# A recommender kernel on one core: masking gathered rows, sharing the last pooling product, two store queues, and another place for eight key transposes

## The chip, the core and the metric

The kernel runs on one core of a Trainium2 chip. A core has five instruction queues that run side by side[...]: TensorE (PE in the profile, with its weight loads shown as PEld), VectorE (DVE), ScalarE (ACT), GpSimd (POOL) and SyncE (SP), which here only issues DMA transfers. ACT and POOL can issue transfers as well. The metric is the device time of one execution in microseconds (us); lower is better.

## What is computed

A batch of 1024 users, each with a history of up to 100 items of 128 numbers, is scored in four parts. Cut to what matters here:

```python
keys = scan(gru_step, h0, history)              # 100 steps, one state of 128 per user and step
score = mlp(concat(keys, q, keys - q, q * keys))  # q: the item; layers of 80, 40, 1, relu
attn = softmax(where(mask == 1, score, -inf), axis=1)
pooled = einsum('bt,btd->bd', attn, keys)       # (users, 128)
att_seq = pooled.T[:100]                        # feature t of pooled weights step t below

def augru_step(h, (x_t, a_t)):                  # x_t: keys of step t, a_t: att_seq[t]
    r = sigmoid([h, x_t] @ Wr)
    u = sigmoid([h, x_t] @ Wu)
    h_hat = tanh([h * r, x_t] @ Wh)
    u = a_t * u
    return (1 - u) * h + u * h_hat

state = aug_seq[length - 1]                     # the state at each user's last step
out = mlp(concat(user, item, hist, item * hist, state))   # 200, 80, 1, sigmoid
```

The second recurrence needs `pooled`, which needs the softmax over all 100 steps, so it can't begin before the first recurrence has ended. A weight `a_t` of zero leaves a state as it is: the kernel therefore sets the weights at and after a user's length to zero, and the last state is then the one that is asked for.

## The kernel before

The batch lies in two halves of 512 users (`HB`), features on the 128 partitions. The work has two phases, and in each of them the order of instructions on every engine is the order in which the code emits them.

The first phase (`gru_phase`) loops over the 100 steps. In each step it runs the GRU of both halves, the attention network of an earlier step (`attend`, matrix products on PE into PSUM, and `take`, which adds the item's part `q0` on DVE and applies relu on ACT), a piece of an online softmax and a piece of the pooling (`pool`). Both networks' products are cut into 32-column pieces, so that four run side by side in the array. Scores go by a small DMA from a row of `mv` to a tile `s_b`, where DVE transposes them. The softmax works in blocks of steps, whose ends are `ENDS` (the last are 93, 96, 98, 100); each block has three stages, `scores(0)`, `tops` and `sums`, which the function `stage` takes from a list. Pooling multiplies the keys of a step by their weights and adds the product to `pooled`; within the loop GpSimd does this. Other instructions of the loop that take no part of the recurrence are handed out one piece for each step by the generator `load_later` (among them a sort of the users by length, whose result is the index tile `idx`).

After the loop comes a tail that is written out by hand (L915 to L987). It finishes the attention of steps 98 and 99 (`take(T - 2)` to `take(T + 1)`), the last three softmax blocks, the pooling (half 0 on GpSimd, half 1 on DVE) and eight pieces of the final network's first layer (`some`, L922). At its end (L976) DVE multiplies each half of `pooled` by the mask of lengths, `used`, into a tile `t`; SP stores the first 32 features to `pooled_d[0]` and the other 96 to `pooled_d[1]` (those of half 1 here, those of half 0 on ACT's queue at L1402).

The second phase (`augru_phase`) is built in three versions for different distributions of lengths. A value in memory, `over_d`, is read by each engine, and a branch (L1475, L1476) selects one. It sorts the users: the stored keys, and the weights in `pooled_d`, are read back with gathers on GpSimd (`load_row` for keys, `gather_weights` for the first 32 weights), indexed by `idx`. Its steps alternate between the halves (`half_step(t, i)`): PE closes the gates r and u with the state, ACT applies sigmoid, DVE multiplies, PE closes the gate h, ACT applies tanh, and PE opens the three gates of the next step with the next key. Some of the things that precede the steady alternation:

- keys of steps 0 to 3 are gathered early as rows (`rows[0, i]`) and transposed on PE by `load_key`, each followed by a copy on ACT;
- `first_step` computes step 0's gates u and h, which depend on the key alone;
- `open_gates(1, 1)` and `open_gates(1, 0)` open six gates;
- `first_state(i, p)` spreads the weights of step 0 over all partitions by a product with the identity (`weight_row`) and sets the state to weight times u times h; `first_weights` spreads those of step 1; `store_weights` transposes all 32 and stores them to `att_d`, from where each later step reads its own by `load_att`.

```python
def first_state(i, p):
    weight_row(0, i, p)
    u, h = gates[i]
    nc.vector.tensor_mul(p, p, u)
    nc.vector.tensor_mul(h3[i], p, h)
```

## Time and profile before

| what | value |
|---|---|
| median of 3 runs | 2014.82 us (2014.07 to 2015.9) |
| the profiled execution's own time | 2014.8 us |
| its span in the profile | 2013.0 us |
| PE busy | 1986.5 us, 99% of the span |
| DVE, ACT, POOL busy | 83%, 46%, 63% |
| mean TensorE clock granted | 0.993 |

The span runs from the first to the last instruction of the program; the execution's own time has 1.8 us around it. The page gives PE as busy nearly throughout, and within the loop of the first phase, and within the steps of the second, its instructions follow each other without a gap. The 40 slices of the page are 50 us each, too wide for the passage from one phase to the other, which lies near 1380 to 1440 us; tables of shorter stretches and instructions in order of time show it. In those, an instruction's line is start, duration, engine, line of the code, operation, output and inputs; square brackets give the idle time before it and what ended it. Matrix products of this kernel in fp32 appear as two records for each instruction.

### The profile page before, as it was taken

Reading aid. Unit: us, or ns where it says so; the run is one execution under the profiler, and the core shown is the slowest. Engines: PE = TensorE matmul, PEld = TensorE weight load, DVE = VectorE, ACT = ScalarE, POOL = GpSimd, SP = SyncE. Lnnn points to the kernel's source line nnn. Section 1 sums busy time; section 2 is a strip of 40 time slices with the busy share of each in tenths; the row PEclk is TensorE's granted clock in tenths of the full one; section 3 lists DMA queues with packets and bytes.
Section 4 is the critical chain, followed back from the end, with each engine's and each line's share of the span. In section 5 each row is a group of like instructions: output and inputs, shape, how many; then the busy total and the mean of one; then the engine's idle time right before and its main releaser. Section 6 shows DMA issues by size and latency. Waiting matters only on the chain.

```text
span 2013.0 us, 40935 instructions
## 1 busy us (share of the span) xinstructions
PE 1986.5 (99%) x15324; PEld 992.8 (49%) x15324; DVE 1672.2 (83%) x3017; ACT 935.5 (46%) x1679; POOL 1277.1 (63%) x1325
## 2 busy tenths in 40 slices
PE   9999999999999999999999999998899999999998
PEld 2345555555433333333333333334444556678997
DVE  7878999887978887888878898998487777888985
ACT  4444454454444454444444454453334444445553
POOL 0233939669796959595887868898674354445331
PEclk9999999999999999999999999999899999999998
DMA  4442333323334334333333333333343343333331
GB/s 124 98 117 91 107 103 103 92 83 104 115 112 102 120 107 121 115 112 102 111 98 96 107 104 94 107 96 106 102 127 101 97 110 98 93 105 95 85 78 30
DMA packets 242075, 204.84 MB, mean 102 GB/s; under 512 B 59506, under 2 KB 204890, under 8 KB 241866
## 3 DMA queue, kind: packets, MB, share of 16 engines
q1 hardware_dynamic: 227514, 169.37, 30.1%
q0 software_dynamic: 12480, 32.04, 5.7%
q8 instruction: 122, 2.00, 0.4%
q14 instruction: 87, 0.71, 0.1%
q10 hardware_dynamic: 1872, 0.72, 0.1%
HBM read 146.01 MB, written 54.41 MB: 100 GB/s over the span
## 4 chain that ended last, share of the span: by engine, by line
PE 95%; DVE 3%; issue 1%; ACT 1%; ACTq 0%; DVEq 0%
PE ps L534 49%; PE pm L700 17%; PE pr L1131 4%; PE ph L1131 4%; PE pu L1131 4%; PE pr L1127 4%; PE ph L1127 4%; PE pu L1127 4%; PE pr L1204 0%; PE ph L1204 0%; PE p L1324 0%; DVE pu L1155 0%; PE pu L1030 0%; PE pd L243 0%; DVE ps L564 0%
## 5 line engine op out<-in xcount | busy, mean ns | idle before, releaser
L534 PE MATMUL ps<-x,wih 128*32 128x512 f32 x4800 | 775.9, 593 | 0.0
L534 PE MATMUL ps<-hn,whh 128*32 128x512 f32 x4752 | 769.6, 592 | 1.4 <-ACT hn L582 1.4
L534 PEld LDWEIGHTS ps<-x,wih 128*32 128x32 f32 x4800 | 259.0, 110 | 302.0 <-issue 299.1
L534 PEld LDWEIGHTS ps<-hn,whh 128*32 128x32 f32 x4752 | 257.0, 110 | 298.7 <-issue 294.6
L519 POOL TENSOR_TENSOR xm<-x,m 128x512 f32<-128x512 f32 x200 | 236.7, 1183 | 142.2 <-DMA m<-mask_d 82.5
L546 ACT ACTIVATE r<-ps,brz 128x512 f32<-128x512 f32 x200 | 137.5, 688 | 388.4 <-PE ps L534 388.2
L520 POOL TENSOR_TENSOR hist<-hist,xm 128x512 f32<-128x512 f32 x200 | 257.9, 1289 | 15.7
L700 PE MATMUL pm<-hn,wk 128*32 128x512 f32 x1200 | 266.4, 592 | 0.1
L700 PE MATMUL pm<-kq,wkq 128*32 128x512 f32 x1200 | 265.8, 592 | 0.0
L188 POOL DMA_INDIRECT rows<-keys_d,idx_k x218 | 211.4, 970 | 81.4 <-POOL rows L187 46.7
L637 POOL TENSOR_TENSOR pooled<-pooled,kw 128x512 f32<-128x512 f32 x191 | 246.0, 1288 | 15.0
L636 POOL TENSOR_TENSOR kw<-kt,e 128x512 f32<-128x512 f32 x191 | 206.3, 1080 | 70.7 <-DVE e L809 70.6
L565 ACT ACTIVATE ps<-ps,bih 128x512 f32<-128x512 f32 x200 | 132.4, 662 | 225.9 <-DVE ps L564 225.9
L554 DVE SCALAR_TENSOR_TENSOR u<-ps,bhh,r 128x512 f32<-128x512 f32 x198 | 147.6, 746 | 73.2 <-PE ps L534 70.5
L1139 ACT ACTIVATE c<-ph,bh 128x510 f32<-128x510 f32 (+57 forms) x174 | 88.1, 507 | 258.8 <-PE ph L1131 221.3
L700 PE MATMUL pm<-mv,w 128*32 128x512 f32 (+1 forms) x808 | 196.3, 592 | 0.8 <-DVE e L790 0.8
L569 DVE TENSOR_TENSOR d<-hn,ps 128x512 f32<-128x512 f32 x198 | 136.1, 687 | 35.9 <-ACT ps L565 35.5
L570 DVE TENSOR_TENSOR d<-ps,d 128x512 f32<-128x512 f32 x200 | 138.3, 692 | 28.4 <-ACT ps L566 14.0
L187 POOL COPY rows<-rest 128x1 f32<-128x1 f32 x202 | 38.3, 190 | 193.0 <-DVE rest L1168 182.9
L582 ACT COPY hn<-ps 128x512 f32<-128x512 f32 x200 | 116.4, 582 | 92.8 <-DVE kq L576 91.0
L564 DVE TENSOR_TENSOR ps<-ps,u 128x512 f32<-128x512 f32 x200 | 140.0, 700 | 22.4 <-PE ps L534 1.5
L571 DVE TENSOR_TENSOR ps<-ps,d 128x512 f32<-128x512 f32 x200 | 139.9, 699 | 6.8
(228 smaller groups left out, 3120.4 us busy)
## 6 DMA issues: line engine op xcount, KB each, us to landing
x<-in_hist_x SPq DMA_DIRECT2D x210, 256.0 KB
keys_d<-kt SPq DMA_DIRECT2D x48, 1024.0 KB
m<-mask_d SPq DMA_DIRECT2D x200, 128.0 KB
rows<-keys_d,idx_k POOLq DMA_INDIRECT x218
s_b<-mv SPq DMA_DIRECT2D x200, 8.0 KB
keys_d<-kt SPq DMA_DIRECT2D x32, 64.0 KB
mask_i<-in_mask SPq DMA_DIRECT2D x8, 200.0 KB
part_d<-part SPq DMA_DIRECT2D x2, 400.0 KB
```

The source lines that it names most:

```text
L188: nc.gpsimd.indirect_dma_start(out=r[:, at, :], out_offset=None, in_=keys_d[q], in_offset=bass.IndirectOffsetOnAxis(ap=idx_k[:, k, i : i + ...
L519: nc.gpsimd.tensor_mul(d, x, m)
L520: nc.gpsimd.tensor_add(acc, acc, d)
L534: nc.tensor.matmul(p[ts(q, R), :], lhsT=w[:, g, ts(q, R)], rhs=v, start=(j == 0), stop=(j == len(parts) - 1),)
L554: nc.vector.scalar_tensor_tensor(out=u, in0=ph, scalar=bhh[:, 2:3], in1=r, op0=ALU.add, op1=ALU.mult,)
L564: nc.vector.tensor_add(pi, pi, u)
L571: nc.vector.tensor_add(pi, pi, d)
L636: eng.tensor_mul(d, k, w)
L637: eng.tensor_add(acc, acc, d)
L700: nc.tensor.matmul(p[i][s, :], lhsT=w[:, s], rhs=v, start=start, stop=stop)
L1127: nc.tensor.matmul(p, lhsT=m[:, 1, :], rhs=k, start=True, stop=False)
L1131: nc.tensor.matmul(p, lhsT=m[:, 0, :], rhs=v, start=False, stop=True)
```

## The change

It is a bundle of seven edits, all of them around the passage from the first phase to the second.

1. The item's part of the attention network at steps 98 and 99 is added by PE (six more instructions in `attend`), and `take` no longer adds it on DVE; ACT reads PSUM itself.
2. In `sums` of the block that ends at 96, the weights are copied to PSUM first, and the sum of the block and the old sum are made from the copy. The copy that the tail made for DVE's pooling goes.
3. The tail's order: feature pieces are issued later, pooling of half 1 is done in smaller portions between the softmax stages, two early key gathers instead of three come before the last block.
4. DVE takes the last multiplication of half 0's pooling (`product`); GpSimd only adds it.
5. Keys 0 and 1 are transposed, and step 0's gates computed, in the tail and not behind the branch. Key 0 goes to `h3`, key 1 to `hist`, the gates to `item` and `s_bs`.
6. The first 32 features are stored unmasked, straight from `pooled`, by two queues (half 1 by SP, half 0 by ACT). Their mask is applied behind the gather, in `first_state`, from a mask `used_s` in sorted order that is made in the loop; for it a third number, the length, goes through the sort. The other 96 features are masked as before, but stored in step 2 of the second phase, by SP.
7. Keys 2 and 3 are transposed inside steps 1 and 2; `first_weights` of half 0 and the order in step 1 move with them.

```diff
-    idx = const.tile([P, GH, NH * 2], I32, name="idx")
+    idx = const.tile([P, GH, NH * 3], I32, name="idx")
+    used_s = const.tile([P, NH, GH, R], U8, name="used_s")
...
+            nc.gpsimd.tensor_copy(ids[:, :, 2], len_i)
...
+            for i in range(NH):
+                sorted_len = pre.tile([P, GH], F32, name="sorted_len")
+                nc.scalar.copy(sorted_len, idx[:, :, 3 * i + 2])
+                nc.vector.tensor_tensor(
+                    out=used_s[:, i],
+                    in0=sorted_len.unsqueeze(2).to_broadcast([P, GH, R]),
+                    in1=step[:, :R].unsqueeze(1).to_broadcast([P, GH, R]),
+                    op=ALU.is_gt,
+                )
+            yield
...
+            def product(self):
+                e, n, t = self.todo.pop()
+                d = wp.tile([P, KH, R], F32, tag="kw", name="kw")
+                w = e[1][:, self.ks, n].unsqueeze(2).to_broadcast(d.shape)
+                nc.vector.tensor_mul(d, self.kt[t // G][:, :, t % G, :], w)
+                self.todo.append((d, None, t))
...
+            def query(i, *groups):
+                for q in groups:
+                    pack(i, q, wq[i], item[:, halves[i].cols], False, False)
+
             for turn in range(2 * NH):
                 i, j = divmod(turn, 2)
+                if j and T - 2 <= t < T:
+                    query(i, 0, 1)
+                    if i:
+                        query(1, QB[1])
+                        query(0, QB[0])
...
-                if t < T:
+                if t < T - 2:
                     sums.append(wp.tile([P, HB], F32, name="f"))
                     nc.vector.tensor_add(sums[-1], p[half.i], q0[:, half.cols])
...
-                nc.vector.tensor_reduce(den_n, e[:, :, :n], AX.X, ALU.add)
+                f, old = e, None
+                if banks and both[1] is None:
+                    b = banks["e"][0]
+                    f = soft["copy"] = b[:, : NK * rows].rearrange("p (k n) -> p k n", n=rows)
+                    old = b[:, HB - NK :]
+                    nc.vector.tensor_copy(f, e[:, :, :rows])
+                nc.vector.tensor_reduce(den_n, f[:, :, :n], AX.X, ALU.add)
...
         exponents()
         some(0, 1)
-        some(2, 3)
+        some(2)
         take(T - 1)
-        some(2, 3)
+        some(2)
         attend(T)
-        some(4)
+        some(3)
...
         take(T)
-        some(4)
+        some(3)
         attend(T + 1)
-        some(5, 6)
+        some(4, 5)
         stage()
+        exponents()
         take(T + 1)
-        exponents()
-        some(5, 6)
-        some(7)
+        some(4, 5)
+        some(6, 7)
+        halves[1].pool(1, nc.vector)
+        stage()
+        halves[0].pool(T, nc.gpsimd)
+        gather_early(2)
+        halves[1].pool(2, nc.vector)
+        some(6, 7)
+        for n in range(2):
+            for half in halves:
+                k = (h3[half.i], hist[:, half.cols])[n]
+                p = pa.tile([P, HB], F32, tag="a", name="pk")
+                for g in range(GH):
+                    nc.tensor.transpose(
+                        p[:, ts(g, P)], rows[0, half.i][:, g, ts(n, P)], ident
+                    )
+                nc.scalar.copy(k, p)
+                later["key", n, half.i] = k
         for half in halves:
             half.store((T - 1) // G)
-        halves[1].pool(T, nc.vector)
-        stage()
-        gather_early(3)
-        halves[0].pool(T, nc.gpsimd)
-        some(7)
         stage(2)
         exponents()
+        for half in halves:
+            gates = (item[:, half.cols], s_bs[NH * ((soft["j"] - 1) % 2) + half.i])
+            later["gates", half.i] = gates
+            for to, (n, f) in zip(gates, (("u", AF.Sigmoid), ("h", AF.Tanh))):
+                if half.i:
+                    p = banks["f"].pop(0)
+                else:
+                    p = pa.tile([P, HB], F32, tag="a", name=f"p{n}")
+                nc.tensor.matmul(
+                    p,
+                    lhsT=later["w" + n][:, 1, :],
+                    rhs=later["key", 0, half.i],
+                    start=True,
+                    stop=True,
+                )
+                nc.scalar.activation(to, p, f, bias=later["b" + n])
         stage()
+        halves[0].product()
         halves[0].pool(T, nc.gpsimd)
         halves[1].pool(T, nc.vector)
         gather_early(3)
-        for half in reversed(halves):
-            t = blocked(s_bs[NH * (soft["j"] % 2) + half.i])
-            nc.vector.tensor_mul(t, later["used"][:, half.ks, :], pooled[:, half.ks, :])
+        for half, eng in zip(reversed(halves), (nc.sync, nc.scalar)):
...
-            nc.sync.dma_start(out=first[0], in_=t[:R])
+            eng.dma_start(out=first[0], in_=pooled[:R, half.ks, :])
+            t = blocked(s_bs[NH * (soft["j"] % 2) + half.i])
+            nc.vector.tensor_mul(t, later["used"][:, half.ks, :], pooled[:, half.ks, :])
...
-        for to, t in later["att", 1]:
-            nc.sync.dma_start(out=to, in_=t)
...
             nc.vector.tensor_mul(p, p, u)
             nc.vector.tensor_mul(h3[i], p, h)
+            r = sorted_rows[i][:, :, 1:R]
+            nc.vector.tensor_mul(r, r, used_s[:, i, :, 1:])
...
-            if t == 1 and i == 0:
-                store_weights(0, pa.tile([P, HB], F32, tag="a", name="pw"))
-                first_state(1, spare)
-            elif t == 1:
-                first_weights(1, spare)
+            if t == 1:
+                first_weights(i, spare)
+                load_key(2, i)
...
             if t == 1 and i:
                 store_weights(1, spare)
+                load_key(3, 0)
+            elif t == 1:
+                open_state(1, 0)
+                store_weights(0, pa.tile([P, HB], F32, tag="a", name="pw"))
+                first_state(1, spare)
+            elif t == 2 and i == 0:
+                load_key(3, 1)
...
-        for i in range(NH):
-            load_key(0, i, (None, FREE_BANK)[i])
-        gates = [first_step(i) for i in range(NH)]
-        for i in range(NH):
-            load_key(1, i, (FREE_BANK, None)[i])
-        for to, t in later["att", 0]:
-            nc.scalar.dma_start(out=to, in_=t)
+        gates = [later["gates", i] for i in range(NH)]
+        keys.update({(1, i): later["key", 1, i] for i in range(NH)})
         sorted_rows = [gather_weights(i) for i in range(NH)]
-        for k in range(14, KH):
+        for k in range(13, KH):
             load_row(1, 0, k)
-        for i in range(NH):
-            load_key(2, i, (FREE_BANK, None)[i])
         open_gates(1, 1, EARLY_BANKS)
         open_gates(1, 0, LATE_BANKS)
-        for i in range(NH):
-            load_key(3, i)
         spare = bank("spare", EARLY_BANKS[-1])
         first_state(0, pa.tile([P, HB], F32, tag="a", name="first"))
-        first_weights(0, spare)
...
+                if t == FIRST[1] - 2:
+                    for to, of in later["att", i]:
+                        nc.sync.dma_start(out=to, in_=of)
```

## The prediction

> **What bounds the kernel now.** I read the page first: its span and the engines' shares of the chain that ended last.

> ```profile
> span 2013.0 us, 40935 instructions
> ...
> PE 95%; DVE 3%; issue 1%; ACT 1%; ACTq 0%; DVEq 0%
> ```

> TensorE carries 95% of the chain, and the change leaves nearly all its work in place. What can move is the rest, about 100 us of chain, and a table of stretches says where. Columns: busy us of PE, PEld, DVE, ACT, POOL with their counts, granted TensorE clock, DMA share, GB/s.

> ```profile
> 1340.00:1380.00 40.00, 40.00 (x369) 14.86 (x362) 36.90 (x57) 21.08 (x33) 36.80 (x32) 1.00 0.24 71
> 1380.00:1405.00 25.00, 19.97 (x111) 12.61 (x109) 20.69 (x49) 9.58 (x20) 19.32 (x20) 1.00 0.38 112
> 1405.00:1410.00 5.00, 1.94 (x8) 1.57 (x8) 4.35 (x14) 0.23 (x1) 4.84 (x5) 0.61 0.74 238
> 1410.00:1415.00 5.00, 3.84 (x5) 1.73 (x6) 4.79 (x8) 3.07 (x5) 4.70 (x5) 0.50 0.01 3
> ...
> 1428.00:1440.00 12.00, 8.84 (x36) 4.86 (x37) 5.83 (x9) 2.51 (x4) 3.99 (x5) 0.87 0.15 41
> 1440.00:1480.00 40.00, 40.00 (x106) 18.80 (x105) 29.72 (x50) 15.78 (x24) 30.05 (x52) 1.00 0.56 161
> ```

> Before 1380 and after 1440 PE is full. Between them DVE and POOL are full up to 1415, and PE works at half clock for part of it. So the change is worth what it takes from these 60 us. The timeline, engine by engine, shows the steps of the passage:

> ```profile
> 1388.35 1.29 DVE L734 TENSOR_TENSOR f<-pm,q 128x512 f32<-128x512 f32 x2 [2.55 <-PE pm L700]
> ...
> 1402.54 0.72 DVE L786 STREAM_TRANSPOSE last<-s_b 128x512 f32<-128x512 f32 x1
> ...
> 1414.71 1.29 DVE L978 TENSOR_TENSOR s_b<-used,pooled 128x512 f32<-128x512 uint8 x2
> 1429.23 0.70 DVE L1064 TENSOR_TENSOR first<-first,first_u 128x512 f32<-128x512 f32 x1 [13.22 <-PE first L1053]
> ```
> ```profile
> 1413.23 1.27 POOL L637 TENSOR_TENSOR pooled<-pooled,kw 128x512 f32<-128x512 f32 x1
> 1414.65 0.98 POOL L188 DMA_INDIRECT rows<-keys_d,idx_k  x1
> ...
> 1420.67 0.95 POOL L153 DMA_INDIRECT att_r<-pooled_d,idx  x1 [2.51 <-DMA pooled_d<-s_b]
> ```
> ```profile
> 1415.43 0.93 SPq L982 DMA_DIRECT2D pooled_d<-s_b  x2
> ```

> DVE is without a break from 1388.35; both poolings end near 1414.6; the mask follows, the two stores start at 1415.43, and the first weight gather waits for the second store until 1420.67. PE's `first` comes at 1427.83, 7.16 us after that gather, and PE is full again some 12 us later. The printed chain runs through PE's key transposes at 1407 to 1427 instead. Both end together: `first` waits for the last row gather of half 0 as well, by its own semaphore, so both branches have to become shorter.

> [...]

> ```profile
> L813 DVE TENSOR_TENSOR old<-den,e x13: 860/866/1023, 301.9 to 1391.2; 128x32 f32<-128x32 f32 x13
> L813 DVE TENSOR_TENSOR old<-den,last x2: 186/187/188, 1402.0 to 1406.4; 128x32 f32<-128x32 f32 x2
> ```

> The same tiny product takes 866 ns from SBUF beside GpSimd and 187 ns from PSUM. [...]ACT's branch at 1406.43 is followed by 3.53 us in which it does nothing, and PE's takes 6.9 us (1400.35 to 1407.28). [...]the table shows 0.50 at 1410 to 1415. [...]

> **The change, part by part.** Times are of the profiled execution (2014.8, practically the median 2014.82); the sum is a shift of PE's full phase.

> *Item part on PE.* 16 instructions become 22. Before, one `attend` at full packing takes 3.43 us: eight records of 0.43 us in each of four column groups. Groups 0 and 1 now hold twelve, so 5.13 us: +1.7 us for step 98 and again for 99. The second ran 5.76 us before (1382.49 to 1388.26), because it began before `mv` was there; now `mv` comes early. So PE ends it at 1381.3 + 2.9 (features) + 5.13 = 1389.3 and ACT's relu at about 1390.6, against 1390.3: +0.3. In exchange DVE loses 4 x 0.65 us of sums, and no longer waits 2.55 us for PE: `scores(0)` starts at 1381.7, the sums at 1386.4 against 1390.8.

> *Copy in PSUM.* L813 and L814 were 1.02 and 1.29 us here and become 0.19 each: -1.9 us on DVE. The copy (0.28) was there already.

> *Pooling order.* The next block's scores need `s_b`, landed at 1392.1 before (DVE came at 1395.8); now 1392.5, and DVE is ready: start at 1391.9. From there: scores and maxima 3.0, one product and sum 1.4, sums 1.1, five pooling instructions 3.6, so the last block starts at 1401.1, against 1402.54. It needs 3.0 to the exponent. ACT now has four key copies of 0.58 before that exponent, PE's features ending at 1401.8: it comes at 1404.75, +0.5. Then 0.3 for the exponent and 1.84 for the sums: 1406.95. `product` 0.7; seven instead of ten instructions of 0.7 for half 1: DVE ends at 1412.7 (before 1414.7, masked half 1 at 1415.4). POOL: 1.07 + 2.36 + 1.28, from 1407 at once: 1411.7 (before 1414.5).

> *Stores.* Each waited for a DVE mask of 0.69 us and for the other one on SP. Now one on each queue at 1412.75 and 1411.8. The first landed 2.7 us after issue, the second 3.8 with three others behind it. I take 2.7: 1415.45. Behind ACT's store, which waits for POOL's last sum, stand its branch and nothing needed before `first`. The big key stores (two of 1 MB, from 1398 to 1409 at 294 GB/s) now follow features and key copies on SP: 1402.6 to about 1411.5, just clear. POOL has three key gathers of 1.26 us first: 1415.4. With 0.8 us from landing to gather as before (1419.86 to 1420.67), the weight gather starts at 1416.2: **-4.45 us**. `first` at 1423.3.

> *PE before `first`.* Four transposes, four gate products and their ACT work (a table load of 1.28, four activations of 0.69) move into the wait for the pooling, free. After the gates (1407.8) PE branches, 6 to 7 us by the row above: 1414. Six openings, four at half clock (1.7) and two at 0.86: 1422.5. Cover 0.8 us, small.

> *From `first` to full PE.* Before: 17.87 us to the product pr of step 2 at 1445.70, of which the waits at 1429.9 to 1434.8, where PE's completions came late by up to 2.9 us beside an instruction fetch at 1432.4, and half-clock products at 1438 to 1440. New, engine by engine: state at +2.85, mask 0.25 (124 elements; nearest row L813 to L790, 0.2 to 0.9), r at +4.65 to 5.35, weights and rest to +7.6, `att_t` +8.25, state of half 1 at +9.7; PE then needs two products 1.7, weights 0.86, two key transposes 0.9, openings 2.6, `store_weights` 0.45, ph 0.86: +17.1. Gain 0.7. Key 3 of half 1 adds 0.45 in the full phase. An instruction fetch that falls into it again costs up to 3 (taken: 0, both ends kept)[...].

> *The rest.* Six stores in step 2 on SP (0.5 to 1.3 us each) stand before loads needed a step later, 10 us: 0. The used_s work in the loop is 4 tiny instructions under full PE; ACT waits once for DVE ahead of the next r: 0 to 0.7, taken 0.2. Fewer early gathers: the third row comes later, needed at 1460: 0.

> Sum: -4.45 - 0.7 + 0.45 + 0.2 = -4.5: 2014.8 - 4.5 = **2010.3 us**.

> **Rivals.** *PE late behind its branch* (23%): [...]the openings all run cold; `first` at 1426.5 and 3 us of the gain is gone: 2013.3. For it: 0.8 us of cover[...]. *The late completions don't return anywhere* (14%), neither here nor at 1388 (where they came 1.0 late), and step 98's products pack better than counted: 2 to 3 us more, 2007.8. *Stores in the way* (8%): [...] If the 2.4 MB move at half of the 294 GB/s, they last 17 us, to 1420, the weights land at 1423, gathers begin at 1424 and `first` comes at 1431: +3.2; with three key transposes of steps 1 and 2 exposed at 1.2 us each (0.44 on PE, 0.58 on ACT, two hand-overs) and the small terms, about 2021. It decides from a landing after 1420. That an edit doesn't do what it says is possible for `product`: it moves 1.07 us from POOL to DVE, and by my sum DVE ends last; without it DVE would end at 1412.0 and POOL at 1412.8, so it is worth nothing either way.

> **How the numbers follow.** My own case has 55%, with a range of 2008.8 to 2012.3[...]. About 0.2% (4 us, below 2010.8) is what this measurement tells from no change; of the 55%, 44 lie below. Faster 44 + 14 = 58%, same 11 + 23 = 34%, slower 8%. The range that holds 8 in 10 leaves out most of the slow case and the best of the fast one: 2007.8 to 2013.6.

> **What would show it.** `scores(0)` of the last block near 1401, the two pooled stores at 1412 to 1413 on two queues, the first weight gather near 1416, `first` near 1423 and the first opening of step 2's products without a late completion. Wrong if `first` waits for PE's openings, if pooled ends after 1414, or if landing takes over 4 us.

## The result, and the profile after

| series | before, median | changed kernel, median | ratio, 95% interval |
|---|---|---|---|
| first (14 and 14 runs) | 2014.85 us | 2012.76 us (2010.76 to 2014.21) | .9990 (.9983 to .9998) |
| second (39 and 19 runs) | 2013.12 us | 2011.24 us (2009.1 to 2014.74) | .9988 (.9981 to .9995) |
| third (47 and 13 runs) | 2005.38 us | 2005.52 us (2000.87 to 2007.02) | .9998 (.9990 to 1.0006) |

The forecast was 2010.3 us, 4.5 us below before. The first two series give 2 us, and the third, on another chip, nothing. The second and third series ran on chips that I call A and C; the first has the level of chip A and profiles like it. Four experiments ran on a chip B, where before takes 2004.94 us; the changed kernel itself did not run there. Of its 13 runs on chip C two took 2000.9 and 2001.3 us and the others 2004.4 to 2007.0, so a profile shows one outcome of several.

The first profile of the changed kernel is that of its fastest run of the first series (2010.76 us). Its page, span and chain by engine:

```profile
span 2009.0 us, 40971 instructions
...
PE 97%; issue 1%; DVE 1%; DMA 0%; ACT 0%; POOL 0%; another core or an unknown queue 0%; SPq 0%; ACTq 0%; DVEq 0%; POOLq 0%
```

The chain names PE with a larger share than before (97% in place of 95%). The table of stretches, with the columns as before:

```profile
1380.00:1405.00 25.00, 24.52 (x142) 15.21 (x141) 20.43 (x57) 13.51 (x27) 20.71 (x19) 1.00 0.32 96
1405.00:1410.00 5.00, 0.77 (x2) 0.00 (x0) 4.83 (x8) 1.49 (x3) 4.65 (x5) 0.89 0.93 286
1410.00:1415.00 5.00, 3.79 (x5) 1.77 (x6) 1.31 (x3) 0.00 (x0) 3.85 (x4) 0.50 0.52 119
1415.00:1428.00 13.00, 10.84 (x34) 5.68 (x33) 2.27 (x4) 1.32 (x2) 9.54 (x10) 0.84 0.14 32
1428.00:1440.00 12.00, 7.39 (x36) 4.70 (x37) 6.84 (x11) 4.05 (x7) 5.13 (x10) 1.00 0.36 104
```

PE does in 1380 to 1405 what it did later before (24.52 us busy, before 19.97), and DVE is done soon after 1410. The stretch at 1428 to 1440 has got worse: PE is busy for 7.39 of 12 us, before for 8.84. The instructions in order of time say why:

```profile
1398.62 0.72 DVE L818 STREAM_TRANSPOSE last<-s_b 128x512 f32<-128x512 f32 x1
1408.58 1.26 POOL L636 TENSOR_TENSOR pooled<-pooled,kw 128x512 f32<-128x512 f32 x1
1409.33 0.69 DVE L652 TENSOR_TENSOR pooled<-pooled,last 128x512 f32<-128x512 f32 x1
1409.87 0.34 ACTq L1045 DMA_DIRECT2D pooled_d<-pooled  x1
1410.05 0.33 SPq L1045 DMA_DIRECT2D pooled_d<-pooled  x1
1410.06 1.29 DVE L1047 TENSOR_TENSOR s_b<-used,pooled 128x512 f32<-128x512 uint8 x2
1412.55 0.96 POOL L189 DMA_INDIRECT rows<-keys_d,idx_k  x1 [0.30 <-issue]
1413.81 0.95 POOL L154 DMA_INDIRECT att_r<-pooled_d,idx  x1 [0.30 <-issue]
1419.86 0.49 PE L1099 MATMUL first<-ident,att_r 128*128 128x128 f32 x2 [0.35 <-DMA att_r<-pooled_d,idx]
1420.48 0.70 DVE L1110 TENSOR_TENSOR first<-first,item 128x512 f32<-128x512 f32 x1 [9.13 <-PE first L1099]
1429.97 0.59 ACT L1118 COPY at<-spare 128x512 f32<-128x512 f32 x1 [4.13 <-remote]
1430.59 0.70 DVE L1211 TENSOR_TENSOR pu<-pu,at 128x510 f32<-128x510 f32 x1 [5.67 <-ACT at L1118]
```

Up to DVE's first product on `first` all is earlier: 1420.48 in place of 1429.23. Nine microseconds later ACT has waited 4.13 us for a product of PE, and DVE 5.67 us for ACT. By its record PE had ended that product (the weights of step 1, `spare`) at 1426.5, but the trace has its semaphore moving only at 1429.91, with six more of PE's moves right behind it, and ACT started at 1429.97. I call this late completions. The profile before had them at 1429.9 to 1434.8.

Since the loop's end differs by up to 3.3 us between the profiles, all that follows counts from one point that the change doesn't touch, the first attention product of step 98 on PE (1375.17 in the first profile before, 1373.55 in the first after). "pr (2, 1)" is the product that closes gate r in step 2, half 1; PE is full from there on. The expectations below call it pr of step 3.

| us from that point | before, A | before, C | changed, A | changed, C | predicted |
|---|---|---|---|---|---|
| scores of the block that ends at 98 | 20.6, 20.5 | 19.5 | 16.4, 16.4 | 16.3 | 16.7 |
| scores of the last block | 27.4, 27.3 | 26.3 | 25.1, 25.1 | 24.9 | 25.9 |
| DVE's pooling ends | 39.5, 39.4 | 38.4 | 36.5, 36.5 | 36.4 | 37.5 |
| first weight gather | 45.5, 45.1 | 43.6 | 40.3, 40.3 | 40.1 | 41.0 |
| DVE's first product on `first` | 54.1, 54.5 | 51.7 | 46.9, 47.1 | 47.0 | 49.6 |
| pr (2, 0) | 70.5, 69.8 | 64.6 | 68.0, 68.0 | 65.4 | 65.2 |
| pr (2, 1) | 75.6, 74.9 | 69.7 | 73.5, 73.5 | 70.9 | 70.8 |

The predicted column is the prediction's own times less 1375.17; its 4.5 us are taken off 1429.23 for DVE's product, its 17.1 us from `first` to pr give pr (2, 0), and pr (2, 1) follows by 5.09 us as before and 0.45 for key 3.

### The profile page after: what moved, and what is told of

It is laid out like the page before. It is cut to its first block, busy times and chain, and to the rows that moved or that the text cites. A ratio compares the mean times of both kernels' runs of the same rounds, so it can differ in the third digit from the quotient of the medians.

```text
span 2009.0 us, 40971 instructions
## 1 busy us (share of the span) xinstructions
PE 1985.1 (99%) x15348; PEld 1079.5 (54%) x15348; DVE 1670.9 (83%) x3018; ACT 936.4 (47%) x1681; POOL 1277.7 (64%) x1325
## 4 chain that ended last, share of the span: by engine, by line
PE 97%; issue 1%; DVE 1%; DMA 0%; ACT 0%; POOL 0%; another core or an unknown queue 0%; SPq 0%; ACTq 0%; DVEq 0%; POOLq 0%
PE ps L546 51%; PE pm L723 18%; PE ph L1179 4%; PE pr L1179 4%; PE pu L1179 4%; PE ph L1175 4%; PE pr L1175 4%; PE pu L1175 4%; PE last L690 1%; PE pr L1257 0%; PE ph L1257 0%; DMA item<-in_item 0%; PE p L1377 0%; DMA bm<-in_b 0%
## 5 line engine op out<-in xcount | busy, mean ns | idle before, releaser
L546 PE MATMUL ps<-x,wih 128*32 128x512 f32 x4800 | 764.0, 593 | 0.0
L546 PE MATMUL ps<-hn,whh 128*32 128x512 f32 x4752 | 757.9, 592 | 1.4 <-ACT hn L594 1.4
L546 PEld LDWEIGHTS ps<-x,wih 128*32 128x32 f32 x4800 | 266.7, 110 | 269.6 <-issue 220.2
L546 PEld LDWEIGHTS ps<-hn,whh 128*32 128x32 f32 x4752 | 264.4, 110 | 266.4 <-issue 215.8
L532 POOL TENSOR_TENSOR hist<-hist,xm 128x512 f32<-128x512 f32 x200 | 258.2, 1291 | 15.7
L723 PE MATMUL pm<-hn,wk 128*32 128x512 f32 x1200 | 254.5, 592 | 0.7 <-issue 0.7
L723 PE MATMUL pm<-kq,wkq 128*32 128x512 f32 x1200 | 254.4, 592 | 0.0
L652 POOL TENSOR_TENSOR pooled<-pooled,kw 128x512 f32<-128x512 f32 x190 | 244.4, 1286 | 14.9
L566 DVE SCALAR_TENSOR_TENSOR u<-ps,bhh,r 128x512 f32<-128x512 f32 x198 | 147.5, 745 | 70.8 <-PE ps L546 68.4
L188 POOL COPY rows<-rest 128x1 f32<-128x1 f32 x202 | 38.5, 190 | 193.0 <-DVE rest L1214 185.0
```

Source lines behind the costliest of these rows:

```text
L532: nc.gpsimd.tensor_add(acc, acc, d)
L546: nc.tensor.matmul(p[ts(q, R), :], lhsT=w[:, g, ts(q, R)], rhs=v, start=(j == 0), stop=(j == len(parts) - 1),)
L566: nc.vector.scalar_tensor_tensor(out=u, in0=ph, scalar=bhh[:, 2:3], in1=r, op0=ALU.add, op1=ALU.mult,)
L652: eng.tensor_add(acc, acc, d)
L723: nc.tensor.matmul(p[i][s, :], lhsT=w[:, s], rhs=v, start=start, stop=stop)
```

## The experiments

The first question was where the earlier weights were lost again. Theory A: the transposes and copies moved into steps 1 and 2 stand in the start's chain. Theory B: PE falls to half clock (granted 0.50 at 1410 to 1415 in the table above), and its late completions come wherever the start then is.

**Keys ahead of `first`.** The second run is on chip C.

```diff
+        for t in (2, 3):
+            for i in range(NH):
+                load_key(t, i, (None, EARLY_BANKS[-1])[i])
         spare = bank("spare", EARLY_BANKS[-1])
...
                 first_weights(i, spare)
-                load_key(2, i)
...
-                load_key(3, 0)
...
-            elif t == 2 and i == 0:
-                load_key(3, 1)
```

> The changed kernel, with keys 2 and 3 transposed ahead of `first` again, as before, alternating two PSUM banks. Reference is the changed kernel's profile: first product of `first` and `first_u` on DVE at 1420.5, the product pr of step 2 at 1441.5, 21.0 us between them (before: 1429.2, 1445.7, 16.5 us). Theory A (moved work: the three transposes and four copies now in steps 1 and 2 stand on the path of the start): the stretch falls to about 17 us, `first` comes up to 1.5 us later, and the kernel gains 2 to 3 us on the changed one: ratio to before about .9977. Theory B (cold clock and PE's late completions, wherever they fall): the stretch stays at 19 to 21 us, and with the later `first` the kernel is 0 to 1.5 us slower than the changed one: ratio .999 to 1.0000.

Measured: 2002.36 us, ratio .9989 (.9981 to .9998) on chip B. DVE's product comes at +49.4, later than expected, and pr (2, 0) 14.9 us after it, pr (2, 1) 20.0 us after it. No completion is late.

**No item part on PE.**

```diff
-                if j and T - 2 <= t < T:
-                    query(i, 0, 1)
...
-                if t < T - 2:
+                if t < T:
```

> The changed kernel without the item part on PE: DVE adds it to the attention sums of steps 98 and 99 again. If the hand-over's gain rests on DVE (the prediction's case), DVE does 4 x 0.65 us more and waits for PE again, the last block's scores come 2 to 4 us later than 1398.6, and the kernel loses 2 to 3.5 us on the changed one: ratio to before 1.000 to 1.001. Rival: the sums of the blocks wait for the landing of s_b anyway (in the changed kernel DVE waits 1.65 us there), and the loss is under 1 us: ratio .999 to .9995.

Measured: 2006.27 us, ratio 1.0006 (.9998 to 1.0014). The scores of the block that ends at 98 come at +18.0 (changed kernel 16.3), the gather at +41.2, DVE's product at +48.1: the 1.8 us at the scores shrink to 1.2, since DVE's wait for the last exponent, 1.01 us in the changed kernel, is 0.30 here. Set against the changed kernel's .9998 on chip C the loss is some 1.6 us, between the two expectations; across two chips this is an estimate.

**Weight gathers first.**

```diff
-        gather_early(3)
...
-        for k in range(13, KH):
+        for k in range(10, KH):
             load_row(1, 0, k)
```

> The changed kernel, with the last three early key gathers behind the weight gathers on GpSimd instead of ahead of them. The changed kernel's stores landed at 1412.05 and 1412.40, and the first weight gather was issued at 1413.81, directly behind the third key gather. If GpSimd's own gathers bind: first weight gather at 1412.6 to 1413.0, the fourth landing about 1 us earlier, `first` 0.6 to 1.0 us earlier (PE's openings end at 1418.7, which stops it there), total -0.8 us against the changed kernel. Rival: the start eats it (late completions stay where they are in time, PE still cold): first product on DVE earlier, pr of step 2 not; total 0.

Measured: 2003.3 us, ratio .9991 (.9983 to .9999). The gather comes at +39.8 and DVE's product at +46.4: 0.4 and 0.5 us earlier than in the changed kernel. GpSimd's own key gathers hid little, for the last store landed at +38.7, only 1.1 us ahead of the gather. pr (2, 1) comes at +69.6, 1.3 us earlier than in the changed kernel on chip C.

**No `product`.**

```diff
-        halves[0].product()
```

> The changed kernel without `product`: GpSimd multiplies and adds the last row itself. The prediction's working gave 0 either way. By the changed kernel's trace GpSimd's chain (last sum 1409.84, three key gathers to 1413.5, weight gather at once) is what the weight gather waits for: 1.07 us more on GpSimd puts that gather at 1414.9 and the total at +1.0 us against the changed kernel. It serves as a second look at the start as well: theory A says 21 us again from the first product on DVE to pr of step 2; theory B lets it differ by the 2 to 3 us of a burst.

Measured: 2007.27 us, ratio 1.0011 (1.0004 to 1.0017). GpSimd in this kernel, in order of time:

```profile
1408.14 1.67 POOL L652 TENSOR_TENSOR pooled<-pooled,kw 128x512 f32<-128x512 f32 x1
1409.96 1.44 POOL L189 DMA_INDIRECT rows<-keys_d,idx_k  x1 [0.15 <-issue]
...
1414.23 0.95 POOL L154 DMA_INDIRECT att_r<-pooled_d,idx  x1 [0.30 <-issue]
```

The last sum takes 1.67 us (one of DVE's masks runs beside it) and the first key gather 1.44 us, in place of 1.26 and 0.99. With the 1.07 us of the multiplication this makes the 1.9 us by which the gather comes later (+42.0). DVE's product is at +49.1. The prediction had called this edit worth nothing.

The stretch from DVE's product to pr (2, 0) is 17.5 us in these three kernels and has no late completions, against 21.1 in the first profile after. So the next series ran both kernels again.

**Both kernels again, on chip A.** The kernels are unchanged.

> The kernel before, profiled once more on the chip of the other three, so that its stretches can be compared with theirs. Counted from the first product of step 98's attention on PE (1375.17 in its first profile), that profile has the first weight gather at +45.5, the first product on DVE of `first` at +54.1 and the product pr of step 3 at +75.6. If the run's spread of 2 to 4 us comes from PE's clock and late completions in the start, the first two come again within 0.5 us and the third differs by up to 4 us.

> The changed kernel, profiled once more. Its first profile has, from the same point, the first weight gather at +40.3, the first product on DVE at +46.9 and pr of step 3 at +73.5, with seven of PE's completions together 2.1 us late at 1429.9. If that late burst belongs to the change, it is there again and the third figure stays at 73 to 74. If it falls by chance, the third figure comes to 69.5 to 71.5, as in the kernels with other small edits (17.5 us from the first product on DVE to pr of step 2 in three of them). Ratio to before .9985 to .9995.

Measured: before's profile (2016.52 us, above all of its 39 other runs on this chip) has the gather at +45.1, DVE's product at +54.5 and pr (2, 1) at +74.9; ACT's copy of `spare` starts 4.3 us behind the end of the product in PE's record. The changed kernel's has +40.3, +47.1 and +73.5: the same as its first profile to 0.1 us. ACT in the second profile of the changed kernel:

```profile
1429.23 0.59 ACT L1118 COPY at<-spare 128x512 f32<-128x512 f32 x1 [4.22 <-remote]
```

So the late completions aren't chance. That left the layout of the kernel or the chip.

**Work for PE that computes nothing.**

```diff
         spare = bank("spare", EARLY_BANKS[-1])
+        filler(1)
         first_state(0, pa.tile([P, HB], F32, tag="a", name="first"))
+        filler(3)
```

`filler(n)` multiplies `wr` with 256 columns of key 1 into `spare`, n times.

> The changed kernel with work added on PE that computes nothing: a product of 128x256 into the free bank ahead of `first`, and three behind it (0.43 us each at full clock), in the 1 to 3 us in which PE waits for the gathers and for DVE. Theory A (the moved transposes and copies lengthen the chain of steps 1 and 2): the stretch from the first product on DVE to pr of step 2 stays at 17.5 us or gets up to 0.4 longer, total 0 to +0.5 us. Theory B (PE stands idle there, its granted clock falls to half, 0.50 at 1420 to 1425 in two of the kernels, and the first products of step 1 run at half speed): clock 0.9 to 1.00 at 1420 to 1425, the stretch 15 to 16 us, total 1.5 to 2.5 us faster than the changed kernel in spite of the added work.

Measured: 2014.41 us, ratio 1.0006 (.9997 to 1.0014), on chip A, where the changed kernel took 2011.24. Its table of stretches, columns as above:

```profile
1415.00:1420.00 5.00, 5.00 (x20) 2.97 (x20) 0.15 (x1) 0.00 (x0) 3.78 (x5) 0.95 0.09 16
1420.00:1425.00 5.00, 4.17 (x21) 2.53 (x19) 1.43 (x3) 0.00 (x0) 3.78 (x5) 1.00 0.11 30
1425.00:1430.00 5.00, 0.00 (x0) 0.00 (x0) 0.32 (x1) 1.01 (x2) 1.06 (x2) 0.91 0.20 58
```

The clock is 1.00 where it was 0.72 in the changed kernel on this chip, as theory B said, and PE's record ends key 2's transposes 4.8 us after DVE's product, in place of 6.5. But then nothing goes on: the trace has one move of PE's semaphore between 1419.73 and 1428.9, ACT starts the sigmoid of pr at 1428.98, 6.5 us after the end of that product in PE's record, and PE stands idle for all of 1425 to 1430. What the clock gave, the late completions took back with more.

**Key transposes as cover.** Key gathers behind the weight gathers, and:

```diff
+        load_key(2, 0)
+        load_key(2, 1, EARLY_BANKS[-1])
         first_state(0, pa.tile([P, HB], F32, tag="a", name="first"))
+        load_key(3, 0, EARLY_BANKS[-1])
+        spare = bank("spare", EARLY_BANKS[-1])
```

> The changed kernel with the last three key gathers behind the weight gathers, keys 2 of both halves transposed ahead of `first` and key 3 of half 0 straight behind it, while PE waits for DVE's state; key 3 of half 1 stays in step 2. By both theories this takes the three transposes out of step 1. A: 1.5 to 2 us less in the stretch from the first product on DVE to pr of step 2, clock no matter. B: the same transposes also fill PE's wait, and the clock is 1.00 at 1415 to 1425: stretch 14.5 to 15.5 us, first product on DVE at +46.5 to +47.5. Total 2 to 3 us faster than the changed kernel, ratio to before .9975 to .998. Rival: as with all three transposes ahead of `first`, half of the runs stay 4 us slower than the others, and the median gains 1 us at most.

Measured: 2015.75 us, ratio 1.0011 (1.0003 to 1.0019), chip A. Every expectation failed, the rival's too. DVE and PE of this kernel in order of time:

```profile
1428.46 0.69 DVE L1211 SCALAR_TENSOR_TENSOR rest<-pu,h_all 128x510 f32<-128x510 f32 x1
1437.70 0.68 DVE L1124 COPY att_t<-pw 32x512 f32<-32x512 f32 x1 [8.55 <-issue]
1440.03 2.07 PE L1177 MATMUL pr<-h_all,wr 128*128 128x510 f32 x2 [10.59 <-DVE h_all L1109]
```

PE's record of `pw` ends at 1428.6, but DVE reads it only at 1437.70, 9.1 us later. The openings began 2.5 us sooner than in the changed kernel and ended by 1413.5, so PE was idle again around `first`, and the clock is 0.50 at 1420 to 1425 all the same.

**Both kernels and keys ahead, on chip C.** All three had run before, but never together.

> The kernel before once more, for its profile beside the other three on their chip. The runs so far fell on two chips: the profiles of both kernels on one of them (before 2013 to 2015 us) have PE completions 2 to 5 us late in the start of the second phase, the four variants on the other (before 2004.9 us) have none. If the late completions belong to the chip, this profile has them or not as the other three have, and without them the stretch from the first product on DVE to pr of step 2, half 1, is 17 to 19 us, not 20.4 to 21.6.

> The changed kernel once more, beside keys_ahead and before on one chip. If the chip has no late completions: first product on DVE at +46.9 from the first attention product of step 98, pr of step 2, half 1, 23 us later (as in the three variants with step 1 unchanged), ratio to before .999 to 1.0000. If it has them: +46.9, then 26.5 us, ratio .999 as in the two series so far.

> The changed kernel with keys 2 and 3 transposed ahead of `first`, once more, since it and the changed kernel ran on different chips. Where the stretch to pr of step 2, half 1, is 20 us (as in its first profile) against 23 without late completions, the kernel is 1 to 3 us faster than the changed one on the same chip, ratio to it about .999. If this chip has late completions: whether they come here too tells if they belong to the chip (they do) or to the layout of the changed kernel's start (they don't).

Measured: before 2005.0 us in one run, changed 2005.52, ratio .9998 (.9990 to 1.0006), keys ahead 2002.68, ratio .9989 (.9982 to .9996). None of the three has a late completion, nor has any of the five other profiles from chips B and C; all six from A and the first series have them. Before needs 17.9 us from DVE's product to pr (2, 1) here, the changed kernel 23.9, keys ahead 20.0. The kernel before, DVE, ACT and PE in order of time:

```profile
1424.83 0.70 DVE L1064 TENSOR_TENSOR first<-first,first_u 128x512 f32<-128x512 f32 x1 [11.98 <-PE first L1053]
1425.62 0.58 ACT L1070 COPY at<-spare 128x512 f32<-128x512 f32 x1 [2.14 <-PE spare L1053]
1426.31 1.12 PE L1131 MATMUL pr<-h_all,wr 128*128 128x510 f32 x2 [0.72 <-DVE h_all L1065]
1429.66 0.70 DVE L1064 TENSOR_TENSOR spare<-spare,first_u 128x512 f32<-128x512 f32 x1 [0.21 <-PE spare L1053]
```

The same with keys ahead:

```profile
1422.57 0.70 DVE L1110 TENSOR_TENSOR first<-first,item 128x512 f32<-128x512 f32 x1 [11.80 <-PE first L1099]
1424.05 1.12 PE L1179 MATMUL pr<-h_all,wr 128*128 128x510 f32 x2 [1.61 <-DVE h_all L1111]
1426.95 0.59 ACT L1118 COPY at<-spare 128x512 f32<-128x512 f32 x1 [0.23 <-PE spare L1099]
1427.57 0.70 DVE L1210 TENSOR_TENSOR pu<-pu,at 128x510 f32<-128x510 f32 x1 [0.98 <-ACT at L1118]
1429.51 0.68 DVE L1110 TENSOR_TENSOR spare<-spare,item 128x512 f32<-128x512 f32 x1
```

And in the changed kernel:

```profile
1421.40 2.07 PE L1179 MATMUL pr<-h_all,wr 128*128 128x510 f32 x2 [1.62 <-DVE h_all L1111]
1423.26 1.91 PE L1179 MATMUL pu<-h_all,wu 128*128 128x510 f32 x2
1424.96 1.75 PE L1099 MATMUL spare<-ident,att_r 128*128 128x128 f32 x8
1426.74 0.58 ACT L1118 COPY at<-spare 128x512 f32<-128x512 f32 x1 [0.88 <-PE spare L1099]
1427.36 0.70 DVE L1211 TENSOR_TENSOR pu<-pu,at 128x510 f32<-128x510 f32 x1 [2.42 <-ACT at L1118]
1429.41 0.70 DVE L1110 TENSOR_TENSOR spare<-spare,item 128x512 f32<-128x512 f32 x1
```

The state of half 1 begins with DVE's product on `spare`. Before, that is 4.83 us after the product on `first`: the weights of step 1 were spread ahead of pr and copied by ACT while PE waited for the state. With keys ahead it is 6.94 us: the copy comes behind pr and pu, and two products of DVE stand ahead of the state. In the changed kernel it is 9.50 us (DVE's first product is at 1419.91): pr, pu and the weights' product run at half clock (2.07, 1.91 and 1.75 us in place of 1.12, 1.02 and 1.05), and ACT and DVE wait for them. The changed kernel's stretches, the clock third from the end:

```profile
1415.00:1420.00 5.00, 2.31 (x9) 1.19 (x8) 0.09 (x1) 0.00 (x0) 3.78 (x5) 0.96 0.08 14
1420.00:1425.00 5.00, 3.60 (x5) 1.55 (x6) 2.18 (x4) 0.66 (x1) 3.78 (x5) 0.50 0.11 21
```

The same two with keys ahead:

```profile
1415.00:1420.00 5.00, 4.71 (x17) 2.42 (x15) 0.00 (x0) 0.68 (x2) 3.78 (x5) 0.88 0.09 16
1420.00:1425.00 5.00, 3.21 (x18) 2.24 (x19) 1.58 (x3) 1.45 (x3) 3.78 (x5) 1.00 0.08 16
```

PE is busy for 2.31 us in 1415 to 1420 in the one and 4.71 in the other; the clock of the next 5 us is 0.50 and 1.00. Behind that, the interval from pr (1, 1) to pr (2, 0) is 7.42 us in place of 6.55, and to pr (2, 1) another 5.53 in place of 5.09: the transposes of step 1 and 2. So both theories hold, each with its part.

This pair differs in one thing more. PE's branch took 5.4 us in the changed kernel and 7.6 us with keys ahead (in all 14 profiles it is 5.2 to 5.7 or 6.8 to 7.7), so that the openings ended at 1415.3 in the one and at 1418.8 in the other. On chip B two kernels had the same long branch, weights first without the four key transposes ahead of `first` and keys ahead with them: the clock of 1420 to 1425 is 0.66 and 1.00, and the state of half 1 begins 8.73 and 6.94 us after DVE's product on `first`. So the transposes do keep the clock up, but part of the 9.50 us goes with the early branch.

Nor is all of the gain of keys ahead in the start. Of the 2.9 us between these two profiles some 1.2 are there; the other 1.7 lie at the end of the program, where the changed kernel (first row) falls to half clock earlier than keys ahead (second row):

```profile
1990.00:1995.00 5.00, 4.73 (x23) 4.54 (x22) 1.67 (x8) 1.47 (x5) 0.80 (x1) 0.50 0.08 28
1990.00:1995.00 5.00, 4.04 (x24) 3.21 (x23) 1.63 (x8) 1.86 (x6) 0.00 (x0) 0.81 0.09 28
```

From pr (2, 1) to the issue of the last store the changed kernel takes 557.6 us, and keys ahead 555.9 on both chips. Whether the edit or only the place of the half-clock stretch in time does this, no run shows.

**Masks ahead of the stores, both on SP's queue.**

```diff
-            eng.dma_start(out=first[0], in_=pooled[:R, half.ks, :])
             t = blocked(s_bs[NH * (soft["j"] % 2) + half.i])
             nc.vector.tensor_mul(t, later["used"][:, half.ks, :], pooled[:, half.ks, :])
+            nc.sync.dma_start(out=first[0], in_=t[:R])
```

> The changed kernel with the masks on DVE ahead of the two pooled stores again, both on SP's queue. The prediction's working: half 1's store comes 0.7 us later (1410.1 to 1410.8), half 0's follows two masks and the other store, 1411.5, and lands near 1414.2 in place of 1412.4. GpSimd's three key gathers end at 1413.5 and hide all but 0.7 to 1.5 us of it: first weight gather at +41 to +41.8 in place of +40.3, total +0.7 to 1.5 us against the changed kernel. Rival: the later gather leaves PE idle longer ahead of `first`, as in no_product, where 1.8 us on the gather cost 2 us or more: total +2 to +3 us.

Measured: 2007.68 us, ratio 1.0012 (1.0005 to 1.0018), chip C. SP's queue and GpSimd in this kernel:

```profile
1409.39 0.93 SPq L1047 DMA_DIRECT2D pooled_d<-s_b  x2
...
1415.57 0.95 POOL L154 DMA_INDIRECT att_r<-pooled_d,idx  x1 [3.46 <-DMA pooled_d<-s_b]
```

The second store goes out at 1409.99, some 1.3 us later than the changed kernel's last, and its last part lands at 1414.76, 4.8 us after issue; from two queues the changed kernel's landed 2.3 and 2.4 us after issue on this chip, and from SP's queue before's took 3.0 and 3.4. The key stores stand ahead on SP's queue in the changed kernel too, so they alone don't explain it. GpSimd waits 3.46 us, the gather comes at +43.3, 3.2 us late, DVE's product 3.1 us late. The rival was right in the total (2.2 us on medians), by another route: most of it is the landing (2.4 us later, beside 1.3 at the issue). Queue and masked tile were changed together, and the run doesn't part them.

## Why the prediction came out as it did

In the first two series the direction held and the time lies in the range, but the gain was 2 us and not 4.5. The sum was made of a gain that is real and a comparison that wasn't sound, and that the time still fell into the range is in part luck: errors of opposite sign, and a chip on which before has late completions of its own.

**The hand-over** was sized rightly in its steps. The tiny sums on DVE of the block that ends at 96 were to take 0.19 us each and do (third row; the second of them, L853, takes 186 ns):

```profile
L852 DVE TENSOR_TENSOR old<-den,e x12: 858/859/1028, 301.1 to 1360.7; 128x32 f32<-128x32 f32 x12
L852 DVE TENSOR_TENSOR old<-den,last x2: 186/187/188, 1394.7 to 1403.2; 128x32 f32<-128x32 f32 x2
L852 DVE TENSOR_TENSOR last<-den,last x1: 196/196/196, 1385.9 to 1385.9; 128x32 f32<-128x32 f32 x1
```

(min, median and max in ns; the first row is the loop's, from SBUF, the second was in PSUM before). Scores, pooling and gather come 0.3 to 1.2 us earlier than predicted. The stores land after 2.2 and 2.4 us in place of 2.7, at 1412.40, and what the gather follows at once is GpSimd's third key gather. The gather's gain of 4.45 us was measured as 5.2 and 4.8 on chip A and 3.5 on chip C. `product` was priced at nothing and gave 1.9 us of gather time on chip B: the prediction compared when the poolings end, and left out that GpSimd's key gathers follow its last sum (by its own times 1412.8 and three of 1.26, 1416.6, where it had the weight gather at 1416.2). Edits 2, 3 and 5 were not undone one at a time; what they gave is read from the times.

**From the gather to DVE's product on `first`** the prediction carried 8.56 us over unchanged. It was 6.7 to 6.8. "Both branches have to become shorter" was right, and both did: PE was to leave its branch at 1414 and end its openings at 1422.5, but left at 1411.2 and ended at 1418.8. This is 1.8 us better than the sum. The rival of PE late behind its branch didn't happen, and neither did that of the key stores in the way: they begin at 1400.43, and the pooled stores behind them land in 2.2 and 2.4 us, though on two queues only.

**From `first` to full PE** is where it failed: "Gain 0.7", from 17.87 us (counted from PE's `first`) to 17.1. Two terms were wrong.

- The base. Of the 17.87 us, the prediction itself named the completions late by 2.9 us, and then took none for the new start ("taken: 0, both ends kept"). On chip A they returned, in both profiles of the changed kernel: the stretch from DVE's product to pr (2, 0) is 21.1 and 20.9 us, before 16.5 and 15.3, predicted 15.7. On chip C neither kernel has them, so that before needs only 12.9 us there, and there was no late completion for the change to lose. The prediction put a start with them beside one without; none of the chips does.
- The clock. All products of step 1 were counted at full clock, with half clock only for the openings. Without the key transposes PE waits around `first` (busy 2.31 of 5 us on chip C) and then 1.6 us for the state, and pr, pu and the weights run at half clock (0.50 at 1420 to 1425, after 5 us in which PE was 46% busy). The trace's record of the clock has the changed kernel at half clock for 6.83 us from 1419.58 on chip C and for 3.41 us from 1422.60 in its first profile; up to the last one of a program, which the end cuts off, every half-clock stretch of the 14 profiles lasts 3.41 us or a multiple of it. A low share of busy time doesn't stand ahead of every one: the stretch at the end of the program, above, begins after 5 us in which PE's record is busy for 4.95. The price is 9.50 less 6.94 us, 2.6 us on chip C, less 0.43 for key 2's transpose: 2.1 us. By the same sum it is 1.4 us for weights first on chip B, whose stretch is 3.41 us.

With its own terms for moved work the prediction was close: keys ahead has pr (2, 0) 14.9 us after DVE's product, and the prediction's 15.7 has two key transposes more, at 0.45 us each. Its 0.45 us for key 3 is measured as 0.44. On chip C DVE's product is 2.6 us ahead of the prediction, the stretch to pr (2, 0) 2.7 us longer (18.4 for 15.7), and so the predicted place of pr (2, 1), +70.8, is met at +70.9 by two errors that cancel, while before stands there at +69.7 and not at +75.6. On chip A the late completions put pr (2, 1) at 73.5, 2.7 us behind the prediction, and only before's own leave a gain of 1.4 to 2.1 us.

The rest was small, as predicted: the work added to the loop shows nothing beyond the spread of the profiles (the point we count from is at 1373.10 before and 1372.96 after on chip C), and the stretch from pr (2, 1) to the issue of the last store is 557.6 us in both there, and 559.5 and 559.1 in the first profiles. In the second profiles on chip A it is 563.8 and 560.6, with a half-clock stretch of 6.83 us near 1972 in before.

What moved, in these profiles, is thus this. The change brings the weights 5 to 7 us earlier, by DVE's product on `first`. On chip C it spends 2.1 us on the order in step 1 (weights behind pr and pu, and DVE's products of half 0 ahead of the state of half 1), about 2.1 us on the clock, and 1.7 us on transposes now in steps 1 and 2 (0.43, 0.87 and 0.44). With keys 2 and 3 transposed ahead of `first` as before, the clock and the transposes' time come back and DVE's product comes 2.5 us later; that leaves some 1.3 us at pr (2, 1). The kernel is at .9989 on two chips, 2.8 us below the changed kernel where both ran (medians 2002.68 and 2005.52), the rest of it at the end of the program. That is the best version of those tried; on chip A it hasn't run.

**What stays open** is the cause of the late completions. Where they come, the trace also holds only half of the landings of DMA transfers in the second phase (713 and 730 events from 1400 to 1500 us for the changed kernel in the first profile and on A, 1428 on C), and fewer moves of PE's semaphore than instructions that make them (2055 for 2240 in the first profile, 2241 on C). In the four profiles of the changed kernel and its variants the held-back completions come 0.7 to 1.0 us after the last recorded landing of the gathers that GpSimd issued without waiting; in the two of before they don't. No run here shows what holds them back, or whether the missing events have the same cause. Before's instruction fetch, which the prediction suspected, isn't needed: in the changed kernel's first profile no instruction fetch at all lies between 1416.4 and 1439.1.

## What to carry to other kernels

A stall in the profile that no instruction of the kernel explains belongs to the base and to the forecast alike: take it out of both, or leave it in both, and look at a second chip before you book its end as a gain. Work that is moved off PE while it waits may have been keeping its clock up (1.00 granted at 1420 to 1425 with the key transposes, 0.50 without, on chip C; 1.00 and 0.66 on chip B); ask what fills the gap that it leaves. And read a gain of two or three microseconds to the end of the program before you credit it to the place of the edit. Where an engine's wait is shortened at one end, count the next chain with the order in which it will issue, since what stood ahead of it in the wait now stands inside it.
